# A first product of four batches in two levels: 49 quarter products for 56 in a graph network kernel

## The chip, the cores and the metric

The kernel runs on one core of a Trainium2 chip. The metric is the device time of one execution in microseconds; the median of three runs before the change is 1519.04 us.

## The reference

The input is x of shape (32, 512, 128): 32 batches, 512 nodes, 128 channels, all f32. Two layers follow each other.

```
# layer 0: both adjacency arguments are adj, so the K=7 taps fold to 4
x = layernorm(x + sum_k (adj^k x) W_k)          # k = 0..3
# layer 1: five steps of a gated unit over the graph
h = x
for 5 steps:
    m = adj @ h ; av = [m, m]
    u3 = h @ u3_w.T + u3_b
    z = sigmoid(av @ w3_w.T + w3_b + u3)
    r = sigmoid(av @ w4_w.T + w4_b + u3)
    hv = tanh(av @ w5_w.T + w5_b + (r*h) @ u5_w.T + u5_b)
    h = (1 - z)*h + z*hv
x = layernorm(x + h)
```

## The kernel before, in words

**Work and its order.** The batches are handled in 16 pairs. `pair(q, key0)` records all operations of pair q as `Op`s: the engine, a planned duration, what it comes after, which buffers it takes and gives back, and a key. `Plan.run` then plays these durations through once, while the program is built, and emits on each engine the ready operation with the smallest key that can take its buffers. The result is a fixed order for every engine; on the chip the engines run that order and wait on semaphores. Buffers come from the `slots` table (lines 153 to 172), so their counts shape the order as well. `KEYS` (line 24) holds the starting key of each pair, `LONG` (line 25) the step of the key from one of the five steps to the next, `inside` the number of pairs that may be under way.

**Products by seven.** A product of a 2x2 block matrix needs eight block products; the Winograd form needs seven and some sums. `seven` (line 358) issues the seven as PE groups into three PSUM banks. Banks `a` and `c` keep accumulating: after a group, its bank's sum is copied out (ACT) or added to something (DVE) before the next group may add to the same bank. `into` (line 344) says where the four output blocks go. The sums of the operands on the data side are made by POOL (`add`, line 475); those of the constant side (`T` for adj, `wt` for the weights, `at2S` for adj squared) are made once at the start.

**Layer 0** (`layer0`, line 530) of a pair has three such products. The first, through `pair_product` (line 479), is adj times x of the two batches: here the 2x2 blocks are the two batches against the two halves of the nodes. Each of the seven groups is two matmuls with a 128x128 stationary block and 256 moving columns (line 489), so 14 matmuls a pair. Its result goes to the tiles `tT`; x turned to channels goes to `xT`. The second product (line 567) takes `xT` and `tT` with the weights and writes `U` and `Y`. The third (line 626) applies adj squared to `U`, adds `Y`, and `norm` makes `h0`. From pair `FIRST` = 2 on, x and h0 are turned by `turn_nodes`, through DRAM; in pairs 0 and 1 by PE transposes (line 268).

**The five steps** (from line 778). Each step has u3 (line 785), the product with adj by `pair_product`, and the gates (lines 703 to 741). The new h is turned back for the next product by `turn` (line 310): a block transpose on DVE (line 325), four DMA pieces to DRAM (line 317) and one DMA back into `X` (line 323). `ON_PE` (line 23) names pairs whose last steps are turned by PE instead. All DMAs are issued by SP, in the planned order. After the last step POOL adds h to h0 (line 834), `norm` follows, and the result is stored (line 841). `h0` of a pair is thus held in SBUF through all five steps, for this residual. In a pair listed in `ON_PE` the last step is `finish` (line 743) instead, where PE does the sum.

Of the kernel before, what the change touches and what calls it, by code (L numbers as in the profile page):

```python
# [14 lines left out]
P = 128  # L15
# [7 lines left out]
ON_PE = {14: 1, 15: 3}  # L23
KEYS = [20.0, 58.0, 80.0, 110.0, 158.0, 194.0, 216.0, 246.0, 282.0, 312.0, 338.0, 366.0, 396.0, 432.0, 468.0, 480.0]
LONG = 20.0
FIRST = 2
EPS = 1e-5
# [95 lines left out]
def gnn_resnorm_kernel(  # L123
# [26 lines left out]
    def tiles(tag, n, shape=(P, N), pool=work):  # L150
# [4 lines left out]
        d=tiles("d", 6, (NR, R, NR, P), dram),  # L155
        xg=tiles("xg", 2, (P, 2, NK, P)),
        xT=tiles("xT", 4),
        tT=tiles("tT", 4),
        U=tiles("U", 3, (P, NK, 2, P)),
        Y=tiles("Y", 2, (P, 2, NK, P)),  # L160
        h0=tiles("h0", 5, (P, 2, NK, P)),
        hT=tiles("hT", 9),
        X=tiles("X", 5),
        uT=tiles("uT", 5),
        rh=tiles("rh", 4),
        z=tiles("z", 3),
        m=tiles("m", 7),
        S=tiles("S", 3, (P, 7, H, P)),
        v=tiles("v", 5),
        two=[None] * 3,  # L170
        inside=[None] * 10,
# [14 lines left out]
    T = const.tile([P, 4, H, HN], F32, tag="T", name="T")  # L186
    make_identity(nc, ident)
# [35 lines left out]


    w_of = lambda: plan["w0"].rearrange("p k b f -> p (k b f)")[:, : 7 * P]
    w0_in = plan("SP", 0.45, lambda: nc.sync.dma_start(w_of(), w0), take=[("U", "w0")], key=-70.0, late=6.5)

# [9 lines left out]

    w0_ready = plan("DVE", 2.3, layer0_weights, after=[w0_in], give=[("U", "w0")], key=-40.0)

# [289 lines left out]

    def layer0(q, key, entered):  # L530
# [3 lines left out]
        slots = [("S", f"Sx{q}")] + [("tT", f"tT{q}_{b}") for b in range(2)]  # L534
        dst = lambda i, j: plan[f"tT{q}_{i}"][:, j * HN : (j + 1) * HN]
        S_of = lambda i: plan[f"Sx{q}"][:, i]
        got, read = pair_product(lambda b: plan[xg][:, b], False, f"x{q}", dst, S_of, slots, ([xin[0]], [xin[1]]), key)
        read = read[0]
# [17 lines left out]

        U_done, reads, own = [], [], None
        for g in range(2):
            name = f"w{q}_{g}"
            block = lambda i, j, g=g: lambda: plan[f"{('xT', 'tT')[j]}{q}_{i}"][:, g * HN : (g + 1) * HN]  # L560
# [15 lines left out]
            t_in = [got[0][g], got[1][g]]  # L576
# [16 lines left out]
            def dst(i, j, g=g):  # L593
                if j == 0:
                    return plan[f"U{q}"][:, g * H : (g + 1) * H, i, :]
                return plan[f"Y{q}"][:, i, g * H : (g + 1) * H, :]
# [309 lines left out]
```

## Time and profile before

| what | value |
|---|---|
| median of 3 runs | 1519.04 us (1515.84 to 1519.85) |
| profiled execution | 1518.7 us |
| its span | 1516.9 us |
| PE busy | 1502.4 us (99%) |
| DVE busy | 968.9 us (64%) |
| POOL busy | 767.1 us (51%) |
| ACT busy | 750.4 us (49%) |
| hardware DMA queue | 127.93 MB, 31.7% of 16 engines |

The span is the time from the first to the last instruction in the trace of one execution. Busy time of an engine is the time in which at least one of its instructions runs. An f32 matmul leaves two records. The records of matmuls overlap, since they are pipelined, so what one costs is the distance from one start to the next. A group's mean duration says how long a single record lasts. In a line of the timeline the columns are start, duration, engine, line of the kernel, operation, output and input tiles, shapes, count; in square brackets stands how long the engine had been idle and what released it.

### The profile page before, as it was taken

How to read it: one execution, taken by the hardware profiler on the slowest of the kernel's cores; microseconds unless marked ns; L12 is line 12 of the kernel's file. 1: busy time of each engine (PE TensorE's matmuls, PEld its weight loads, DVE VectorE, ACT ScalarE, POOL GpSimd, SP SyncE). 2: the span in 40 equal slices, each digit the busy share in tenths (PEclk: the TensorE clock that was granted, in tenths of full speed). 3: DMA queues.
4: the chain of work that ended last, by engine and by line, in shares of the span. 5: the costliest groups of instructions: out<-in, count | busy, mean ns of one | idle time of the engine just before them, and what ended most of it. 6: DMA issues, size and time to landing. Idle time of an engine off the chain costs nothing.

```text
span 1516.9 us, 20326 instructions
## 1 busy us (share of the span) xinstructions
PE 1502.4 (99%) x6296; PEld 1044.2 (69%) x6296; DVE 968.9 (64%) x2048; ACT 750.4 (49%) x1610; POOL 767.1 (51%) x1082
## 2 busy tenths in 40 slices
PE   8999999999999999999999999999999999999997
PEld 7877666585678666677676767766666686756655
DVE  4455576757674766665776666577476657576665
ACT  3445444536554645445545445455455545555454
POOL 3654354446564645545555554555355564544351
PEclk9999999999999999999999999999999999999999
DMA  3133242334242424234333333334243222423310
GB/s 116 36 98 84 59 109 61 85 77 126 77 107 82 139 62 102 74 87 108 82 86 97 98 84 97 98 79 111 63 108 93 77 57 69 111 65 89 83 42 28
DMA packets 162140, 129.23 MB, mean 85 GB/s; under 512 B 18544, under 2 KB 127088, under 8 KB 162032
## 3 DMA queue, kind: packets, MB, share of 16 engines
q1 hardware_dynamic: 162032, 127.93, 31.7%
q8 instruction: 50, 0.82, 0.3%
q14 instruction: 58, 0.48, 0.1%
HBM read 64.95 MB, written 62.91 MB: 84 GB/s over the span
## 4 chain that ended last, share of the span: by engine, by line
PE 97%; DMA 1%; DVE 1%; POOL 1%; SPq 0%; issue 0%; ACT 0%; ACTq 0%; POOLq 0%; DVEq 0%
PE bank L489 38%; PE bank L703 36%; PE bank L785 9%; PE bank L567 6%; PE bank L626 6%; PE bank L425 1%; PE bank L751 1%; PE bank L268 1%; SPq L317 0%; DMA xg<-in_x 0%; DMA d<-v 0%; DMA v<-d 0%; DVE v L325 0%; POOL rstd L286 0%; DMA X<-d 0%
## 5 line engine op out<-in xcount | busy, mean ns | idle before, releaser
L489 PE MATMUL bank<-T,S 128*128 128x256 f32 x1400 | 346.8, 379 | 0.5 <-ACT tT L350 0.5
L740 POOL TENSOR_TENSOR hT<-z,hT 128x512 f32<-128x512 f32 x156 | 197.6, 1272 | 279.6 <-DVE z L738 277.7
L489 PEld LDWEIGHTS bank<-T,S 128*128 128x128 f32 x1400 | 262.7, 190 | 93.7 <-ACT m L350 35.9
L350 ACT COPY m<-bank 128x256 f32<-128x256 f32 x320 | 119.1, 372 | 266.3 <-PE bank L489 264.6
L489 PE MATMUL bank<-at,S 128*128 128x256 f32 x880 | 224.8, 379 | 1.1 <-ACT S L469 1.1
L354 DVE TENSOR_TENSOR m<-bank,m 128x256 f32<-128x256 f32 x240 | 100.4, 419 | 175.8 <-PE bank L489 116.8
L489 PEld LDWEIGHTS bank<-at,S 128*128 128x128 f32 x880 | 164.7, 190 | 63.0 <-issue 35.6
L736 DVE TENSOR_TENSOR bank<-bank,hT 128x512 f32<-128x512 f32 x156 | 107.5, 694 | 104.2 <-ACT bank L724 103.9
L703 PE MATMUL bank<-m,w4s 128*128 128x512 f32 x320 | 160.5, 592 | 0.0
L703 PE MATMUL bank<-m,w3s 128*128 128x512 f32 x320 | 159.4, 592 | 0.0
L724 ACT ACTIVATE bank<-bank,hv_b 128x512 f32<-128x512 f32 x160 | 105.6, 661 | 108.6 <-PE bank L703 107.5
L785 PE MATMUL bank<-hT,u3s 128*128 128x512 f32 x320 | 159.1, 592 | 0.0
L703 PE MATMUL bank<-m,w5s 128*128 128x512 f32 x320 | 156.9, 592 | 0.0
L703 PE MATMUL bank<-rh,u5s 128*128 128x512 f32 x320 | 156.9, 592 | 0.0
L708 DVE SCALAR_TENSOR_TENSOR bank<-bank,b4s,uT 128x512 f32<-128x512 f32 x160 | 119.9, 752 | 44.2 <-PE bank L703 37.2
L790 ACT ACTIVATE uT<-bank,ub3s 128x512 f32<-128x512 f32 x160 | 109.2, 686 | 64.3 <-PE bank L785 62.3
L710 ACT ACTIVATE bank<-bank 128x512 f32<-128x512 f32 x160 | 93.2, 583 | 92.4 <-DVE bank L708 92.3
L715 DVE SCALAR_TENSOR_TENSOR bank<-bank,b3s,uT 128x512 f32<-128x512 f32 x160 | 119.7, 753 | 27.2 <-PE bank L703 25.6
L717 ACT ACTIVATE z<-bank 128x512 f32<-128x512 f32 x160 | 95.0, 597 | 55.7 <-DVE bank L715 52.1
L325 DVE STREAM_TRANSPOSE v<-hT 128x512 f32<-128x512 f32 x152 | 105.7, 701 | 20.7 <-POOL hT L740 18.3
L711 DVE TENSOR_TENSOR rh<-bank,hT 128x512 f32<-128x512 f32 x160 | 108.0, 679 | 11.4 <-ACT bank L710 10.8
L738 DVE TENSOR_TENSOR z<-bank,z 128x512 f32<-128x512 f32 x156 | 104.9, 681 | 1.8
(129 smaller groups left out, 2190.8 us busy)
## 6 DMA issues: line engine op xcount, KB each, us to landing
d<-v SPq DMA_DIRECT2D x832, 64.0 KB, 1.8
X<-d SPq DMA_DIRECT2D x152, 256.0 KB, 2.8
v<-d SPq DMA_DIRECT2D x56, 256.0 KB, 2.8
xg<-in_x SPq DMA_DIRECT2D x32, 256.0 KB, 3.0
out<-h SPq DMA_DIRECT2D x32, 256.0 KB, 2.1
at<-in_adjT SPq DMA_DIRECT2D x4, 256.0 KB, 4.7
U<-in_w SPq DMA_DIRECT2D x1, 448.0 KB, 6.1
z<-in_w SPq DMA_DIRECT2D x3, 128.0 KB, 5.9
```

Source lines behind the costliest of these rows:

```text
L325: blocks = lambda: nc.vector.transpose(plan[f"v{name}"], src_of())
L350: return "ACT", COPY[cols], lambda src: nc.scalar.copy(dst(i, j), src)
L489: nc.tensor.matmul(dst, lhsT=left[:, k, :], rhs=right[:, k, :], start=(first and k == 0), stop=(last and k == H - 1), skip_group_check=True,)
L703: mm = lambda dst, w, src, first, last: nc.tensor.matmul(plan[dst], lhsT=w, rhs=plan[src], start=first, stop=last)
L708: emit = lambda: nc.vector.scalar_tensor_tensor(plan[pr], plan[pr], b4s, plan[uT], ALU.add, ALU.add)
L711: emit = lambda: nc.vector.tensor_tensor(plan[rh], plan[pr], plan[h], ALU.mult)
L715: emit = lambda: nc.vector.scalar_tensor_tensor(plan[pz], plan[pz], b3s, plan[uT], ALU.add, ALU.add)
L724: emit = lambda: nc.scalar.activation(plan[ph], plan[ph], AF.Tanh, bias=hv_b)
L736: emit = lambda: nc.vector.tensor_tensor(plan[ph], plan[ph], plan[h], ALU.subtract)
L740: emit = lambda: nc.gpsimd.tensor_tensor(plan[h], plan[z], plan[h], ALU.add)
L785: emit = lambda bn=bn, hb=h[b]: nc.tensor.matmul(plan[bn], lhsT=u3s, rhs=plan[hb], start=True, stop=True)
L790: emit = lambda bn=bn, uT=uT: nc.scalar.activation(plan[uT], plan[bn], AF.Identity, bias=ub3s)
```

## The change

The first product of layer 0 is made for two pairs, that is four batches, at a time from pair `SINGLE` = 2 on. The blocks are split twice: the outer level has seven products, of which each is again made by the seven scheme with 128x128 quarters, so 7 x 7 = 49 matmuls of 128 columns stand where 2 x 14 matmuls of 256 columns stood. Four of the outer products run together as batch A (one PSUM bank holds their four quarters of 128 columns), three as batch B. The inner sums lie in the new tiles `SA` and `SB`, those of the constant side in `TT`, made once on DVE. The outer sums of the results go to `M` and to a tile of the new tag `UY`, which replaces `U` and `Y`. Pairs 0 and 1 keep the old product, with its output in `M` instead of `tT`.

`h0` of pairs 0 to 12 is written to DRAM after the first step's product (`hd`) and read back in the last step for the residual. Several buffer counts, `ON_PE`, `KEYS` and `LONG` are changed with it. The diff, cut to its core:

```diff
 STEPS = 5
-ON_PE = {14: 1, 15: 3}
-KEYS = [20.0, 58.0, 80.0, 110.0, 158.0, 194.0, 216.0, 246.0, 282.0, 312.0, 338.0, 366.0, 396.0, 432.0, 468.0, 480.0]
-LONG = 20.0
+ON_PE = {14: 2, 15: 2}
+KEYS = [8.0, 22.0, 60.0, 88.0, 108.0, 144.0, 174.0, 188.0, 210.0, 244.0, 274.0, 310.0, 338.0, 368.0, 384.0, 396.0]
+LONG = 19.0
+KEPT = 3
 FIRST = 2
...
         bank=tiles("bank", 8, pool=psum),
         d=tiles("d", 6, (NR, R, NR, P), dram),
+        hd=tiles("hd", 6, (P, 2, NK, P), dram),
         xg=tiles("xg", 2, (P, 2, NK, P)),
-        xT=tiles("xT", 4),
-        tT=tiles("tT", 4),
-        U=tiles("U", 3, (P, NK, 2, P)),
-        Y=tiles("Y", 2, (P, 2, NK, P)),
-        h0=tiles("h0", 5, (P, 2, NK, P)),
-        hT=tiles("hT", 9),
-        X=tiles("X", 5),
-        uT=tiles("uT", 5),
-        rh=tiles("rh", 4),
+        xT=tiles("xT", 3),
+        M=tiles("M", 1, (P, 4, N)),
+        SA=tiles("SA", 1, (P, 25, P)),
+        SB=tiles("SB", 1, (P, 15, P)),
+        UY=tiles("UY", 2, (P, 4, N)),
+        h0=tiles("h0", 4, (P, 2, NK, P)),
+        hT=tiles("hT", 8),
+        X=tiles("X", 3),
+        uT=tiles("uT", 6),
+        rh=tiles("rh", 2),
         z=tiles("z", 3),
-        m=tiles("m", 7),
-        S=tiles("S", 3, (P, 7, H, P)),
-        v=tiles("v", 5),
+        m=tiles("m", 5),
+        S=tiles("S", 2, (P, 7, H, P)),
+        v=tiles("v", 4),
         two=[None] * 3,
-        inside=[None] * 10,
+        inside=[None] * 14,
     )
     plan = Plan(slots)
...
-    w_of = lambda: plan["w0"].rearrange("p k b f -> p (k b f)")[:, : 7 * P]
-    w0_in = plan("SP", 0.45, lambda: nc.sync.dma_start(w_of(), w0), take=[("U", "w0")], key=-70.0, late=6.5)
+    TT_sums = []
+    for i, n, of in (
+        (0, 4, lambda k, c: T[:, :, k, c]),
+        (4, 2, lambda k, c: at.rearrange("p (o k) c -> p o k c", o=2)[:, :, k, c]),
+        (6, 1, lambda k, c: at[:, H + k : H + k + 1, HN + c.start : HN + c.stop]),
+    ):
+        lo, hi = slice(0, P), slice(P, HN)
+        b11, b12, b21, b22 = of(0, lo), of(0, hi), of(1, lo), of(1, hi)
+        t = lambda j, i=i, n=n: TT[:, i : i + n, j, :]
+        def emit(b11=b11, b12=b12, b21=b21, b22=b22, t=t):
+            for j, (a, b) in enumerate(((b12, b11), (b22, t(0)), (b22, b12), (b21, t(1)))):
+                nc.vector.tensor_tensor(t(j), a, b, ALU.subtract)
...
+    def quad_product(X_of, name, after, key):
+        SA, SB, PA, M = (f"{t}{name}" for t in ("SA", "SB", "PA", "M"))
+        X = lambda i, j, b: lambda: X_of(2 * i + b)[:, j * H : (j + 1) * H]
+        LOW, HIGH = slice(3, 5), slice(5, 7)
+        part = lambda S, at, w: lambda: plan[S][:, at + w.start : at + w.stop]
+        def inner(S, at, a, after):
+            out = lambda i: lambda: plan[S][:, at + i]
+            s2 = add(0.45, out(1), a(0, 0), a(1, 0), ALU.subtract, after, key)
+            s0 = add(0.45, out(3), a(1, 0), a(1, 1), ALU.add, after, key)
+            s1 = add(0.45, out(0), out(3), a(0, 0), ALU.subtract, [s0], key)
+            s3 = add(0.45, out(2), a(0, 1), out(0), ALU.subtract, [s1], key)
+            return s1, s2, s3, s0
+        quarter = lambda i, j: lambda b, k: lambda: X_of(2 * i + b)[:, j * H + k]
+        at_of = {0: 4, 1: 11, 2: 18}
+        own = plan("-", 0.0, lambda: None, after=[o for a in after for o in a], take=[("SA", SA), ("UY", PA)], key=key)
+        s0, s2, s1 = [], [], []
+        for b, w in ((0, HIGH), (1, LOW)):
+            s0.append(add(0.73, part(SA, 11, w), X(1, 0, b), X(1, 1, b), ALU.add, [own], key))
+            s2.append(add(0.73, part(SA, 4, w), X(0, 0, b), X(1, 0, b), ALU.subtract, [own], key))
+            s1.append(add(0.73, part(SA, 18, w), part(SA, 11, w), X(0, 0, b), ALU.subtract, s0[-1:], key))
+        x11 = inner(SA, 0, quarter(0, 0), [own])
+        q = lambda i: lambda: plan[SA][:, 4:].rearrange("p (o b) c -> p o b c", o=3)[:, :, i]
+        ready = s0 + s1 + s2
+        i2 = add(0.98, q(1), q(5), q(3), ALU.subtract, ready, key)
+        i0 = add(0.98, q(3), q(3), q(4), ALU.add, [i2], key)
+        i1 = add(0.98, q(0), q(3), q(5), ALU.subtract, [i0], key)
+        i3 = add(0.98, q(2), q(6), q(0), ALU.subtract, [i1], key)
+        def lefts(S, at, direct):
+            sums = {2: 0, 4: 1, 6: 2, 3: 3}
+            if direct is None:
+                sums = {**sums, 5: 4, 0: 5, 1: 6}
+            return [
+                (lambda i=i: plan[S][:, at + sums[i]])
+                if i in sums
+                else direct(*{0: (0, 0), 1: (0, 1), 5: (1, 1)}[i])
+                for i in range(7)
+            ]
+        def right(block, sums):
+            quarters = {0: (0, 0), 1: (1, 0), 6: (1, 1)}
+            def R_of(i):
+                if i in quarters:
+                    k, c = quarters[i]
+                    return block[:, k, c * P : (c + 1) * P]
+                return TT[:, sums, {2: 1, 3: 0, 4: 2, 5: 3}[i]]
+            return R_of
+        def product(dst, left, i, first, last):
+            for o, (L, R_of) in enumerate(left):
+                nc.tensor.matmul(
+                    dst[:, o],
+                    lhsT=L[i](),
+                    rhs=R_of(i),
+                    start=(first and o == 0),
+                    stop=last,
+                    skip_group_check=True,
+                )
+        def terms(factors, waits):
+            return [(lambda: factors, lambda i=i: i, list(waits.get(i, ()))) for i in range(7)]
+        block = lambda i, j: slice((2 * i + j) * P, (2 * i + j + 1) * P)
+        shape = lambda n: lambda bank: bank[:, : n * P].rearrange("p (o c) -> p o c", o=n)
+        factors = [
+            (lefts(SA, 0, quarter(0, 0)), right(B11, 4)),
+            (lefts(SA, 4, None), right(T[:, 2], 2)),
+            (lefts(SA, 11, None), right(T[:, 0], 0)),
+            (lefts(SA, 18, None), right(T[:, 1], 1)),
+        ]
+        waits = {2: [x11[0], i1], 3: [x11[3], i0], 4: [x11[1], i2], 6: [x11[2], i3]}
+        dst = lambda i, j: plan[PA][:, :, block(i, j)]
+        own = plan("-", 0.0, lambda: None, after=ready, take=[("SB", SB), ("M", M)], key=key)
+        p, ends = seven(
+            f"{name}A", ready + TT_sums, 0.88, terms(factors, waits), product, into(dst, N), key, shape(4)
+        )
+        pA = p
+        x12 = inner(SB, 0, quarter(0, 1), [own])
+        x22 = inner(SB, 4, quarter(1, 1), [own])
+        s3 = [add(0.73, part(SB, 8, HIGH), X(0, 1, 0), part(SA, 18, HIGH), ALU.subtract, [own, *s1], key)]
+        one = slice(4, 5)
+        last = lambda: X_of(1)[:, H + 1 : H + 2]
+        s3.append(add(0.45, part(SB, 8, one), last, part(SA, 18, one), ALU.subtract, [own, *s1], key))
+        four = slice(0, 4)
+        all4 = list(x12) + [i0, i1, i2, i3]
+        s3.append(add(1.27, part(SB, 8, four), part(SB, 0, four), part(SA, 18, four), ALU.subtract, all4, key))
+        plan("-", 0.0, lambda: None, after=pA + s3, give=[("SA", SA)], key=key)
+        factors = [
+            (lefts(SB, 0, quarter(0, 1)), right(B21, 5)),
+            (lefts(SB, 4, quarter(1, 1)), right(T[:, 3], 3)),
+            (lefts(SB, 8, None), right(B22, 6)),
+        ]
+        dstB = lambda i, j: plan[M][:, :3, block(i, j)]
+        plus = lambda i, j: plan[PA][:, :3, block(i, j)]
+        pB, endsB = seven(
+            f"{name}B",
+            s3 + list(x22) + ends,
+            0.66,
+            terms(factors, {}),
+            product,
+            into(dstB, 3 * P, plus),
+            key,
+            shape(3),
+            give=[("SB", SB)],
+        )
+        def dve(d, a, b, after):
+            emit = lambda: nc.vector.tensor_tensor(d(), a(), b(), ALU.add)
+            return plan("DVE", 0.69, emit, after=after, key=key)
+        PA_of = lambda o: lambda: plan[PA][:, o]
+        M_of = lambda o: lambda: plan[M][:, o]
+        u = dve(PA_of(3), PA_of(3), PA_of(0), ends)
+        v = dve(M_of(3), PA_of(1), PA_of(2), ends + [own])
+        e22 = dve(M_of(3), M_of(3), PA_of(3), [u, v])
+        e12 = dve(M_of(2), M_of(2), PA_of(3), [u] + endsB)
+        e21 = dve(M_of(1), M_of(1), PA_of(3), [u] + endsB)
+        plan("-", 0.0, lambda: None, after=endsB + [e12, e21, e22], give=[("UY", PA)], key=key)
+        read = pA + pB + s3 + list(x11 + x12 + x22) + s0 + s1 + s2
+        return [endsB + [e12], endsB + [e12], [e21, e22], [e21, e22]], [read] * 4
+    in_quad, t_reads = {}, {}
     def layer0(q, key, entered):
         xin = x_in.get(q) or loaded_x(q, (key, key))
         xg = f"xg{q}"
-        slots = [("S", f"Sx{q}")] + [("tT", f"tT{q}_{b}") for b in range(2)]
-        dst = lambda i, j: plan[f"tT{q}_{i}"][:, j * HN : (j + 1) * HN]
-        S_of = lambda i: plan[f"Sx{q}"][:, i]
-        got, read = pair_product(lambda b: plan[xg][:, b], False, f"x{q}", dst, S_of, slots, ([xin[0]], [xin[1]]), key)
-        read = read[0]
+        quad = q >= SINGLE
+        Mn = f"Mx{q - (q - SINGLE) % 2 if quad else q}"
+        if not quad:
+            dst = lambda i, j: plan[Mn][:, i, j * HN : (j + 1) * HN]
+            S_of = lambda i: plan[f"Sx{q}"][:, i]
+            slots = [("S", f"Sx{q}"), ("M", Mn)]
+            got, read = pair_product(
+                lambda b: plan[xg][:, b], False, f"x{q}", dst, S_of, slots, ([xin[0]], [xin[1]]), key
+            )
+            read = read[0]
+        else:
+            if Mn == f"Mx{q}":
+                other = x_in[q + 1] = loaded_x(q + 1, (key, key))
+                X_of = lambda b: plan[f"xg{q + b // 2}"][:, b % 2]
+                in_quad[q] = quad_product(X_of, f"x{q}", [[o] for o in xin + other], key)
+            i = 2 * ((q - SINGLE) % 2)
+            got, read = (o[i : i + 2] for o in in_quad[q - i // 2])
+            got, read = list(got), read[0] + read[1]
+        def t_block(b, g):
+            if not quad:
+                return plan[Mn][:, b, g * HN : (g + 1) * HN]
+            return plan[Mn][:, 2 * g + (q - SINGLE) % 2, b * HN : (b + 1) * HN]
         x_turned = []
         for b in range(2):
...
+        flat = lambda i: plan[f"UY{q}"][:, 2 * i : 2 * i + 2].rearrange("p k f -> p (k f)")
+        U_of = lambda: flat(0).rearrange("p (k b c) -> p k b c", k=NK, b=2)
+        Y_tile = lambda: flat(1).rearrange("p (b k c) -> p b k c", b=2, k=NK)
         U_done, reads, own = [], [], None
         for g in range(2):
             name = f"w{q}_{g}"
-            block = lambda i, j, g=g: lambda: plan[f"{('xT', 'tT')[j]}{q}_{i}"][:, g * HN : (g + 1) * HN]
+            block = lambda i, j, g=g: lambda: (
+                t_block(i, g) if j else plan[f"xT{q}_{i}"][:, g * HN : (g + 1) * HN]
+            )
             S = lambda i, name=name: lambda: plan[f"S{name}"][:, i].rearrange("p k c -> p (k c)")
             W = lambda i: lambda: wc[:, i, :]
             WT = lambda i: lambda: wt[:, i, :]
...
-            t_in = [got[0][g], got[1][g]]
-            take = [("S", f"S{name}")] + ([("U", f"U{q}"), ("Y", f"Y{q}")] if g == 0 else [])
+            t_in = list(got[0]) + list(got[1]) if quad else [got[0][g], got[1][g]]
+            take = [("S", f"S{name}")] + ([("UY", f"UY{q}")] if g == 0 else [])
             own = plan("-", 0.0, lambda: None, after=x_turned + t_in + [w0_ready, own], take=take, key=key + 8)
             s2 = add(0.73, S(2), block(0, 0), block(1, 0), ALU.subtract, [own], key + 8)
...
             reads += p + [s2, s3]
-        give = [(t, f"{t}{q}_{b}") for t in ("xT", "tT") for b in range(2)]
-        plan("-", 0.0, lambda: None, after=reads, give=give, key=key)
+        plan("-", 0.0, lambda: None, after=reads, give=[("xT", f"xT{q}_{b}") for b in range(2)], key=key)
+        if not quad or Mn != f"Mx{q}":
+            plan("-", 0.0, lambda: None, after=reads + t_reads.pop(Mn, []), give=[("M", Mn)], key=key)
+        else:
+            t_reads[Mn] = reads
         name = f"y{q}"
-        block = lambda i, j: lambda: plan[f"U{q}"][:, i * H : (i + 1) * H, j, :]
+        block = lambda i, j: lambda: U_of()[:, i * H : (i + 1) * H, j, :]
         S = lambda i: lambda: plan[f"Sy{q}"][:, i]
...
             got, read = pair_product(X_of, turned, name, dst, S_of, slots, after, key)
+            if s == 0 and q < NP - KEPT:
+                emit = lambda: nc.sync.dma_start(plan[f"hd{q}"], plan[f"h0{q}"])
+                done = read[0] + read[1] + h_done[0] + h_done[1]
+                t = plan("SP", 0.45, emit, after=done, take=[("hd", f"hd{q}")], key=key + 5, late=2.5)
+                spilt = plan("-", 0.0, lambda: None, after=[t], give=[("h0", f"h0{q}")], key=key)
+            if last and q < NP - KEPT:
+                emit = lambda: nc.sync.dma_start(plan[f"h0{q}"], plan[f"hd{q}"])
+                take, give = [("h0", f"h0{q}")], [("hd", f"hd{q}")]
+                fetched = plan("SP", 0.45, emit, after=[spilt] + got[0], take=take, give=give, key=key + 5, late=3.0)
             if s > 0:
                 for b in range(2):
...
                 )
-                t = plan("POOL", 1.27, emit, after=[t], give=[("X", Xb)], key=key + 17)
+                ready = [t, fetched] if q < NP - KEPT else [t]
+                t = plan("POOL", 1.27, emit, after=ready, give=[("X", Xb)], key=key + 17)
                 i = 2 * q + b
                 y_of = lambda k, y=y: y()[:, k, :]
                 over = norm(NK, f"1_{i}", y_of, y_of, [t], [], key + 17)
```

## The prediction

> **What bounds the kernel now.** I read the page's busy shares first, then the table by stage, then PE's waits, then stretches of PE's timeline for the price of each matmul shape.
>
> ```profile
> PE 1502.4 (99%) x6296; PEld 1044.2 (69%) x6296; DVE 968.9 (64%) x2048; ACT 750.4 (49%) x1610; POOL 767.1 (51%) x1082
> PE 97%; DMA 1%; DVE 1%; POOL 1%; SPq 0%; issue 0%; ACT 0%; ACTq 0%; POOLq 0%; DVEq 0%
> ```
>
> PE is busy 99% of the span and is 97% of the chain that ended last. Where PE is not busy shows in the stage table (window, PE busy and records, then the other engines):
>
> ```profile
> 0.00:12.00 12.00, 7.60 (x27) 6.26 (x28) 3.21 (x6) 3.65 (x6) 3.96 (x10) 1.00 0.68 213
> 50.00:100.00 50.00, 48.39 (x280) 39.47 (x279) 25.95 (x75) 23.94 (x54) 28.90 (x47) 1.00 0.22 59
> 100.00:1400.00 1300.00, 1300.00 (x5342) 893.51 (x5341) 849.54 (x1778) 654.50 (x1410) 673.80 (x944) 1.00 0.34 89
> 1500.00:1517.00 17.00, 8.80 (x51) 6.14 (x49) 9.54 (x29) 7.01 (x16) 2.92 (x6) 0.92 0.16 62
> ```
>
> From 100 to 1400 us PE never stops, at full clock. All idle time is 4.4 us while x arrives, 1.6 us between 50 and 100, 0.4 near 1430, and 8.2 us after the last matmul: 14.5 us. PE's waits agree:
>
> ```profile
> PE bank L268 <- DMA xg<-in_x: 4.4, 2, 3.8
> PE bank L489 <- ACT S L469: 1.1, 1, 1.1
> PE bank L489 <- ACT tT L350: 0.5, 1, 0.5
> PE bank L268 <- POOL hT L740: 0.4, 1, 0.4
> ```
>
> So PE's work in the middle is worth its full time, and other engines' work is worth nothing until it makes PE stop.
>
> The price of a matmul is its pitch, not its mean duration (379 ns and 275 ns overlap their neighbours). Each f32 matmul leaves two records, so x4 of 128x256 are two matmuls and x8 of 128x128 are four, both 512 columns:
>
> ```profile
> 420.03 1.03 PE L489 MATMUL bank<-at,S 128*128 128x256 f32 x4
> 420.90 1.05 PE L626 MATMUL bank<-U,at 128*128 128x128 f32 x8
> 421.79 1.03 PE L489 MATMUL bank<-at,S 128*128 128x256 f32 x4
> 422.65 1.05 PE L626 MATMUL bank<-U,at 128*128 128x128 f32 x8
> 423.54 1.95 PE L626 MATMUL bank<-S,at2S 128*128 128x128 f32 x16
> ```
>
> Start to start: 0.865 us for two 256-column matmuls (0.4325 each), 0.89 us for four of 128 (0.2225 each).
>
> **The change part by part.**
>
> *The matmuls.* Two pairs' first products are 2 x 14 = 28 matmuls of 256 columns: 28 x 0.4325 = 12.11 us. A group of four batches now issues 49 of 128 columns: 49 x 0.2225 = 10.90 us. That is 1.21 us less per group; pairs 2 to 15 make 7 groups: 8.5 us. Columns alone (one eighth fewer) would give 10.5 us; two microseconds go back because short matmuls have the worse pitch. The built program has 343 matmuls at the new line and 196 fewer at L489 (1344 to 1148), so it does what it says; every other kind is unchanged in number.
>
> Here a rule speaks against the change. The trace has 111 ns per 128-column record and 216 ns per 256-column record: halving costs 3%. The Trainium skill ("TensorE: Matmul & The Clock Gate", section "Back-to-back issue gap") gives a stream of weight load and matmul at N=128 about 81 ns each, where the isolated gap is 56 ns, so weight loads should cost 45% more. Estimated by that page, the 49 would cost 49 x 0.4325/2 x 1.45 = 15.4 us, and the change would lose 23 us in all. L626 loads a new 128x128 weight for each 128-column matmul, just as the new product does, and runs at 0.89 us for four. I take the row.
>
> *POOL.* Removed per group: 8 sums of 256 columns at 0.73 = 5.8 us. Added: 25 sums. The rows give 0.73 for 256 columns and 1.27 for 512; on that line 128 cost 0.46 and 384 cost 1.0 (estimates). 7 x 0.73 + 13 x 0.46 + 4 x 1.0 + 1.27 = 16.4 us. So 10.6 more, 74 us over 7 groups: POOL goes from 767 to about 841 us, 56% of the span.
>
> *DVE and ACT.* Removed per group: 6 DVE sums at 0.419 and 8 ACT copies at 0.372. Added: 3 sums of 512 columns out of PSUM (0.69), 7 of 384 (between the 0.42 and 0.69 rows: 0.555), 5 of 512 with both sources in SBUF, and 4 ACT copies at 0.586. The 5 have two prices. Alone such a sum takes 0.68; beside a POOL sum the trace shows
>
> ```profile
> 7.22 1.42 POOL L476 TENSOR_TENSOR S<-xg 128x256 f32<-128x256 f32 x2 [5.93 <-DMA xg<-in_x]
> 7.92 1.27 DVE L220 TENSOR_TENSOR T<-at 128x512 f32<-128x512 f32 x1 [7.06 <-DMA at<-in_adjT]
> 8.60 1.17 POOL L476 TENSOR_TENSOR S<-S,xg 128x256 f32<-128x256 f32 x1
> ```
>
> 1.27 and 1.17 where 0.68 and 0.73 are usual. The Trainium skill ("GPSIMD Engine Reference", section "1. Specifications") says that GpSimd shares its SBUF interfaces with VectorE and meets contention when a DVE instruction has two SBUF inputs; the rows agree. So the 5 cost 3.4 to 6.4 us per group and hold POOL about as much. DVE rises by 48 to 69 us, plus 12 sums for the constant TT once (6 to 8 us, in the first 40 us): about 1030 of 1510 us, 68%. ACT falls by 4. No engine nears PE; I cost all this at nothing between 100 and 1400, because there PE has other pairs' products and gates to issue. What is late if that cover fails is a bank of the long product: its accumulation waits for a 512-column copy (0.59) where it waited for 0.37.
>
> *DRAM for h0.* 13 writes and 13 reads of 512 KB, 13.6 MB on 128; DMA share from 32% to about 35%. No row has this size in the steady state: 256 KB lands in 2.1 to 3.0 us, 448 KB in 6.1 in the crowded start. I take 4, as the two 256 KB rows with their fixed part shared, and keep 2.1 and 6.1. SP issues 26 more at about 0.45: 12 us on a queue that mostly waits (562 us for L325 alone). The read is issued after the last step's first output block and used by the residual sum after gates and turn. The turn alone is 0.70 + 1.76 + 1.8 + 0.35 + 2.8 = 7.4 us, with some 9 us of gates before it, so 4 or 6 us hide. The residual sum on POOL (L834) now waits for this read too; behind it in POOL's order stand other pairs' sums for their next products. Queued behind a late write or read on SP are the turns (L317, L323) of other pairs, for which the next product's copies and sums wait.
>
> *A longer wait.* The second product of either pair (L567) now waits for batches A and B of four batches and the outer sums, not for one pair's seven groups; `SA`, `SB` and `M` exist once, so the next group waits for both pairs' second products. Who waits for that is layer 0 of four batches, while the steps of earlier pairs fill PE; nothing, as long as the keys keep it ahead.
>
> *Fewer buffers, moved starts.* X 5 to 3, rh 4 to 2, m 7 to 5, S 3 to 2, h0 5 to 4. Fewer buffers (all counts in the diff) tie PE's order to later releases. In the new order I followed each release to the PE work that stands before its user at the prices above: away from the ends the shortest distances are the same as before (a copy of 0.37 behind one matmul group), and those gave no wait in the trace. Nothing, then, up to 3 us.
>
> *The start.* Here I charge something. Pairs 0 and 1 now start 14 us apart (before 38), and the first group at key 60. After the last matmul of pair 0's third product only 20 matmuls of 128 columns stand before the transposes of its normalised h0: 4.45 us. In the profile that way took from 52.4 us (the product's end) to 59.6 (the sixth L296): 7.2 us. So 2.7 us of PE idle; before, PE idled 1.6 in that region, and part of it may not return. +1 to +2.7; I take +1.5. TT and the weights are ready before their first users.
>
> *The tail.* ON_PE keeps four steps with PE transposes in all, so PE's count is the same. Pair 15 turns one step more by DMA (7.4 us against about 1.5); pair 14's products and gates, interleaved with it in the new order, stand over that. After the last u5 product five groups of four 128-column matmuls (5 x 0.89) follow in both versions. The two batches' final sums now end back to back instead of 1.8 us apart, so the first statistics start 0.9 later and the last end 0.9 later (8 x 0.4 us on DVE, to 1510.55 before). The batch that ends last is now the one scaled on DVE (1.4 on POOL, 1.33 on DVE) and no longer the one on POOL and ACT (1.8 and 1.5 after the statistics). 0, plus or minus 1.
>
> **Sum.** -8.5 + 1.5 + 0.5 (stray waits) = -6.5. The profiled execution took 1518.7 us (span 1516.9 and 1.8 around it) and is 0.3 below the median, 1519.04. Forecast 1518.7 - 6.5 + 0.3 = 1512.5.
>
> **The rivals.**
>
> *The start costs nothing* (0.15): the first pairs idle as little as before or less, and the saving is whole: 8.5 to 10, so 1509 to 1510.5. For: the start had 1.6 us idle to win. Against: the 20 matmuls above.
>
> *Stray waits eat it* (0.17): fewer buffers, and 512-column copies between accumulations of one bank, give short stops. At 0.3 to 0.9 us per group of four (7 groups), 2 to 6.5 us go and a gain of 0 to 4.5 is left: 1514.5 to 1519. For: POOL and DVE each gain 5% load, and POOL already waits on transfers. Against: 0.00 idle from 100 to 1400 under the same kind of tight places.
>
> *SP's queue becomes the limit* (0.06), slower: a 512 KB write waits on SP for the release of h0's readers, or a read for a free h0 of 4, and the turns of other pairs queue behind. Each of 26 issues would have to stop PE by more than (8.5 - 1.5 + 4.6)/26 = 0.45 us to pass the bound of slower. At 6.1 us landing and 0.8 us of PE each, 21 us lost less 7 won: 1533. Against: SP waits for its producers most of the time, and most turns have over 10 us of PE work between landing and user.
>
> **How the numbers follow.** The likeliest case (0.62) is 1510.5 to 1514.5. 0.3% (4.6 us, about what a measurement of this kernel can tell from no change) puts faster below 1514.5: 0.62 + 0.15 = 0.77; same 0.17; slower 0.06. The range 1508 to 1518 takes in the whole saving with a better start and most of the stray waits.
>
> **What would show it.** PE busy near 1494; four new matmuls at 0.89 us; PE 0.0 idle from 100 to 1400; 3 us idle between 40 and 80; POOL near 840. It is wrong if the four take over 0.95, if PE waits for X, m or SA in the middle, or if PE waits follow the 512 KB transfers.

## Result and the profile after

The changed kernel takes 1511.33 us (median of 5 runs, 1510.59 to 1512.27) where the kernel before takes 1519.04 (5 runs beside it): ratio 0.9955, 95% interval 0.9941 to 0.997. It is 7.7 us faster; the forecast was 6.5. The profiled execution after took 1511.12 us with a span of 1509.3.

The page's busy shares and its chain of what ended last:

```profile
PE 1493.1 (99%) x6590; PEld 1044.1 (69%) x6590; DVE 1021.8 (68%) x2123; ACT 749.1 (50%) x1582; POOL 844.3 (56%) x1201
PE 97%; DMA 1%; DVE 1%; SPq 0%; POOL 0%; ACT 0%; issue 0%; POOLq 0%; DVEq 0%
```

PE is still the bound. It has 294 records more and 9.3 us of busy time less. POOL (predicted 841) and DVE (about 1030) took up the sums. The stage table (window, PE busy and records, PEld, DVE, ACT, POOL, clock, DMA share, GB/s):

```profile
0.00:12.00 12.00, 8.28 (x41) 6.45 (x42) 4.19 (x7) 4.69 (x8) 5.44 (x11) 1.00 0.69 213
12.00:50.00 38.00, 35.68 (x228) 32.62 (x228) 26.01 (x60) 10.08 (x24) 18.49 (x21) 1.00 0.19 56
50.00:100.00 50.00, 48.57 (x279) 38.41 (x277) 26.63 (x68) 26.75 (x57) 37.40 (x62) 1.00 0.23 64
100.00:1400.00 1300.00, 1299.93 (x5657) 901.33 (x5656) 897.62 (x1850) 655.05 (x1386) 742.43 (x1052) 1.00 0.37 99
1500.00:1510.00 10.00, 0.68 (x7) 0.49 (x5) 4.23 (x20) 1.51 (x4) 2.94 (x6) 0.77 0.16 62
```

The middle stays full: 0.07 us idle in 1300. What is new is 2.3 us of idle time between 12 and 50, where the kernel before had 0.02:

```profile
12.00:50.00 38.00, 37.98 (x237) 34.98 (x236) 19.49 (x43) 11.73 (x28) 17.62 (x24) 1.00 0.24 70
```

PE's waits after the change name it (total us, times, longest):

```profile
PE bank L290 <- DMA xg<-in_x: 4.5, 2, 3.6
PE bank L749 <- DVE UY L376: 1.3, 1, 1.3
PE bank L749 <- ACT UY L372: 0.9, 2, 0.5
PE bank L290 <- ACT h L318: 0.4, 1, 0.4
```

The second wait for x (1.0 us at 14) is pair 1's, whose start moved forward. The second product's wait of 1.3 at 27 us is for an add on DVE, which stands in DVE's queue behind four sums for `TT`; the last of them, the add, and PE's matmul:

```profile
25.82 0.94 DVE L241 TENSOR_TENSOR TT<-at,TT 128x256 f32<-128x256 f32 x1
26.68 0.41 DVE L376 TENSOR_TENSOR UY<-bank,UY 128x256 f32<-128x256 f32 x1
27.24 0.68 PE L749 MATMUL bank<-wc,S 128*128 128x128 f32 x4 [1.34 <-DVE UY L376]
```

The two ACT waits are one bank's copies between groups of pair 1's second product, issued back to back. The transposes of h0 wait 0.4.

The new product on PE's timeline, eight records (four matmuls) of 128 columns, and what follows:

```profile
78.58 1.05 PE L615 MATMUL bank<-TT,SA 128*128 128x128 f32 x8
79.47 1.02 PE L888 MATMUL bank<-rh,u5s 128*128 128x512 f32 x2
```

79.47 - 78.58 = 0.89 us, as L626 in the kernel before. The unseen costs, from the groups by shape (busy, mean ns) and the DMA issues (count, size, median us to landing):

```profile
L498 POOL TENSOR_TENSOR SA<-SA 128x384 f32<-128x384 f32 x28 | 28.1, 1003 | 0.7
L672 DVE TENSOR_TENSOR M<-M,UY 128x512 f32<-128x512 f32 x21 | 17.4, 856 | 0.2
hd<-h SPq DMA_DIRECT2D x13, 512.0 KB, 3.9
h<-hd SPq DMA_DIRECT2D x13, 512.0 KB, 3.9
```

### The profile page after: what moved, and what is told of

Same layout as the page of the kernel before. It is cut to its first block, busy times and chain, and to the rows that moved or that the text cites. A ratio compares the mean times of both kernels' runs of the same rounds, so it can differ in the third digit from the quotient of the medians.

```text
span 1509.3 us, 21208 instructions
## 1 busy us (share of the span) xinstructions
PE 1493.1 (99%) x6590; PEld 1044.1 (69%) x6590; DVE 1021.8 (68%) x2123; ACT 749.1 (50%) x1582; POOL 844.3 (56%) x1201
## 4 chain that ended last, share of the span: by engine, by line
PE 97%; DMA 1%; DVE 1%; SPq 0%; POOL 0%; ACT 0%; issue 0%; POOLq 0%; DVEq 0%
PE bank L888 36%; PE bank L511 32%; PE bank L970 9%; PE bank L811 7%; PE bank L749 6%; PE bank L615 5%; PE bank L936 1%; PE bank L447 1%; DMA z<-in_w 0%; PE bank L290 0%; DMA X<-d 0%; DVE TT L241 0%; DMA xg<-in_x 0%; POOL S L498 0%; ACT h L318 0%
## 5 line engine op out<-in xcount | busy, mean ns | idle before, releaser
L511 PE MATMUL bank<-T,S 128*128 128x256 f32 x1232 | 307.1, 379 | 0.2
L511 PEld LDWEIGHTS bank<-T,S 128*128 128x128 f32 x1232 | 228.4, 190 | 75.3 <-ACT m L372 32.0
L511 PE MATMUL bank<-at,S 128*128 128x256 f32 x824 | 211.3, 379 | 0.0
L511 PEld LDWEIGHTS bank<-at,S 128*128 128x128 f32 x824 | 153.4, 190 | 57.4 <-issue 36.7
L376 DVE TENSOR_TENSOR UY<-bank,UY 128x256 f32<-128x256 f32 (+1 forms) x117 | 54.4, 467 | 82.0 <-PE bank L749 36.2
```

The source lines that it names most:

```text
L376: return "DVE", ADD[cols], lambda src: nc.vector.tensor_tensor(dst(i, j), src, dst(i, j), ALU.add)
L511: nc.tensor.matmul(dst, lhsT=left[:, k, :], rhs=right[:, k, :], start=(first and k == 0), stop=(last and k == H - 1), skip_group_check=True,)
```

## Experiments

Twelve kernels ran in three sets. Each has its ratio to the kernel before measured beside it, whose median was 1519.28, 1519.64 and 1519.19 in the three; the last column is the median less 1511.59, the changed kernel's own in the first set.

| kernel | set | median us | ratio to before, 95% | to the changed kernel |
|---|---|---|---|---|
| before_again | 1 | 1519.26 | 1.0002 (0.9993 to 1.001) | +7.7 |
| after_again | 1 | 1511.59 | 0.9946 (0.9934 to 0.9959) | 0 |
| split | 1 | 1530.45 | 1.007 (1.0057 to 1.0084) | +18.9 |
| single | 1 | 1530.15 | 1.0067 (1.0053 to 1.0081) | +18.6 |
| single_oldkeys | 2 | 1535.77 | 1.0108 (1.0093 to 1.0123) | +24.2 |
| keep | 2 | 1532.70 | 1.0093 (1.0079 to 1.0107) | +21.1 |
| spblock | 2 | 1517.93 | 0.9989 (0.9981 to 0.9998) | +6.3 |
| cover | 2 | 1575.68 | 1.0374 (1.0359 to 1.0388) | +64.1 |
| cover_pool | 3 | 1553.51 | 1.0225 (1.0211 to 1.0239) | +41.9 |
| cover_planned | 3 | 1528.22 | 1.0054 (1.0042 to 1.0067) | +16.6 |
| tt_late | 3 | 1519.05 | 0.9999 (0.9991 to 1.0007) | +7.5 |
| start | 3 | 1517.38 | 0.9992 (0.9984 to 1.0001) | +5.8 |

One number besides the views is used below, the *excess*: over all neighbouring matmul records, the time from start to start beyond the median of that line and shape, where it is more than 5 ns. It counts stops, a slow start and broken pace alike. It is 8.1 us before, 8.2 in before_again, 8.2 after and 8.8 in after_again.

**Both kernels again.** before_again and after_again are the two files unchanged.

> The kernel before, once more, for a second trace of its start. Theory (the start differs from run to run): its matmuls in the first 12 us ran at half pace until about 11 us in the first trace and until 6.7 in the trace of after; that is a matter of when the clock rises and not of the kernel, so this trace may show either, and the time goes with it by 1 to 3 us (1516 or 1519). Rival (the order of the start sets it): the second trace shows the half pace until 11 us again.

> The changed kernel, once more. Theory: PE busy 1493 to 1496 by how long the start runs at half pace, the idle of about 7.5 us before 100 us again with the same two stops (near 14 and 27 us), 1511 plus or minus 1.5. Rival (those stops are chance): idle before 100 us falls to the 6.0 of before.

The gain returns (7.7 us between medians). before_again ran at half pace only until 8.7 us where before did until 12.3 (the expectation had read 11), so this differs from run to run. The spans of the two are equal, 1516.9, but by two differences that cancel: before_again loses 2.0 us less in the first 12 us and 1.8 more between 100 and 1400.

In after_again PE stops for the same second product on DVE's `UY` (1.2), the same two ACT copies (0.9) and `h` (0.4); the stop for pair 1's x does not return, and PE's idle time in the first 100 us is 6.6 us, between the 7.5 expected and the rival's 6.0. The stops that return belong to the order, the x stop to the run.

**split: what a shorter matmul costs.** Each of the 1148 matmuls of 256 columns at L511 is issued as two of 128, same columns, one weight load more each.

```
 for k in range(H):
-    nc.tensor.matmul(dst, lhsT=left[:, k, :], rhs=right[:, k, :], ...)
+    for c in range(H):
+        nc.tensor.matmul(dst[:, chunk(c)], lhsT=left[:, k, :], rhs=right[:, k, chunk(c)], ...)
```

> Prices the shape by itself: every matmul of 256 columns in the steps' products and in pairs 0 and 1 becomes two of 128 with the same weights loaded twice; columns and results are the same. 1148 matmuls become 2296. Theory (a 128-column matmul has a pitch of 0.2232 and a 256-column one of 0.4322): 1148 x 0.0142 = 16.3 us more, 1527 to 1529. Rival (a weight load for each 128 columns costs 45%): over 1148 x 0.19 = 220 us more, 1730.

It is 18.9 us slower, 1.5 us above the range of the theory, and 17.7 by the spans of the profiled executions: 15.4 to 16.5 ns for each split, about 4% of a 256-column matmul. The page:

```profile
PE 1511.2 (99%) x8886; PEld 1123.2 (74%) x8886; DVE 1020.6 (67%) x2123; ACT 749.2 (49%) x1582; POOL 842.3 (55%) x1201
```

The weight loads rise only to 74% busy and stay hidden. By the stream of the Trainium skill ("TensorE: Matmul & The Clock Gate", section "Back-to-back issue gap"), 81 ns at 128 columns where the isolated gap is 56, 45% more, an estimate for this run is some 220 us; here the measurement decides, as the row did in the forecast.

**single: the old product inside the new kernel.** `SINGLE` = 16 sends every pair through `pair_product`; the tiles `SA` and `SB` go, `M` gets a second buffer, all else (keys, buffers, h0 in DRAM) stays.

> Undoes the products alone: every pair makes its first product by the old 14 matmuls of 256 columns; the keys, ON_PE, h0 in DRAM and the smaller buffers stay as in after (M twice, since a pair needs its own). Theory (the gain is PE's columns at their pitch): PE busy 8.2 more than after, time 1519 to 1521. Rival (the new order and buffers give part of the gain): clearly under 1517. Second rival (the old product fits these keys badly): idle between 100 and 1400, over 1524.

The second rival came true: 18.6 us slower. The excess is 19.3 where after_again has 8.8, so 10.5 us are stops and broken pace, and 8.2 of the 18.7 between the spans are left for the columns, the product's own difference. What is left is by the meaning of the excess no more than the counts times the usual distances, so it is no second proof of the forecast's 8.5; the distances themselves are what split tests. But the old product in these surroundings is 11 us slower than in the kernel before.

**single_oldkeys: single with the old schedule.** Also takes the start keys, `LONG`, `ON_PE` and the limit of pairs inside from the kernel before.

> The old first product everywhere, with the old keys, LONG, ON_PE and the limit of 10 pairs, but with the smaller buffers and with h0 in DRAM as in after. The run single lost 11 us to stops of PE that after doesn't have. Theory (those stops come from keys that were chosen for groups of four; buffers and DRAM cost nothing): 1518 to 1521, and PE's stops between 100 and 1400 under 2 us. Rival (fewer buffers stop PE when the short products don't relieve it): over 1524, with waits for m, S or X in the middle.

1535.8, slower still by 5.6. My theory that the keys alone made single slow fell. The rival's time came (over 1524), not its place: of an excess of 26.3, 12.2 us lie between 50 and 100 us. The old keys were chosen for the old buffers; with the new, fewer ones and the trip to DRAM they stop PE more. Which of these does it was not separated.

**keep: h0 not sent to DRAM.** `KEPT` = 16, with the same 4 buffers of h0, no tile `hd`.

> h0 stays in SBUF for all pairs (no write to DRAM, no read back) with the four h0 buffers of after. What DRAM is for: with h0 kept, at most four pairs are between layer 0's end and their store. Theory (the transfers cost nothing and buy buffers): slower than after, since a pair of the next group must wait with its third product until an older pair has stored: 3 to 20 us. Rival (the transfers cost time, or the fifth buffer isn't needed): equal or faster, 1508 to 1512.

21 us slower, just beyond the theory's 3 to 20. PE is idle 4.2 us between 100 and 400 and 2.8 between 1450 and 1500, and its waits are many small ones:

```profile
PE bank L510 <- ACT m L371: 3.7, 8, 0.5
PE bank L289 <- POOL hT L924: 3.5, 2, 1.9
PE bank L748 <- ACT UY L371: 2.8, 6, 0.5
```

As I read them: a pair that waits for an h0 buffer starts late, fewer pairs are on the way, and PE runs one pair's groups back to back, where each waits for the copy before it; that chain was not traced. With these keys and four buffers of h0, the changed kernel without the trip to DRAM is slower than the kernel before.

**spblock: SP held up.** Each of the 13 reads of h0 is issued twice, so SP waits for the first to land before the second.

```
+nc.sync.dma_start(plan[f"h0{q}"], plan[f"hd{q}"])
 nc.sync.dma_start(plan[f"h0{q}"], plan[f"hd{q}"])
```

> The rival of the SP queue: each of the 13 reads of h0 is issued twice in a row into the same buffer, so the second waits on SP for the first to land (about 4 us), with all other transfers behind it. PE's order is unchanged. Theory (the turns behind it have mostly over 10 us until their users): under 2 us slower than after, 1511 to 1513.5. Rival (SP's queue is near its limit): 13 x 4 us x some part reaches PE, 10 us or more slower, over 1521.

6.3 us slower, between the two. SP's own waits show the block, 46.2 us in 13 times, 3.6 on average:

```profile
SPq L990 <- DMA h<-hd: 46.2, 13, 5.1
```

PE then waits in two places more, L511 on `m` (2.4) and on `S` (2.0), where the changed kernel has none. By which of the queued transfers each came late was not traced, and the doubled reads also move 6.8 MB more, which was not separated from the block. 6.3 / 13 = 0.5 us for each read: of 46 us of block most is absorbed, not all.

**cover: do the sums have room?** In the outer step of each group, `s0` and `s2` are computed three times over on POOL and `v` five times on DVE. PE's order is the same, and the planner is not told.

```
-s0.append(add(0.73, part(SA, 11, w), X(1, 0, b), X(1, 1, b), ALU.add, [own], key))
+s0.append(add(0.73, part(SA, 11, w), X(1, 0, b), X(1, 1, b), ALU.add, [own], key, 3))
 ...                                  # s2 likewise, v five times
```

> Takes away cover: in each group of four the four outer sums s0 and s2 run three times on POOL (8 more of 256 columns, 5.8 us per group) and one outer result sum runs five times on DVE (4 more of 512 columns, 2.7 to 5 us per group), with the same results and the same order on all engines. POOL about +41 us, DVE about +20 to 35. Theory (only PE's columns count; the sums have room): time within 1.5 us of after, 1511 to 1513. Rival (the sums' load is near what stops PE): 3 to 8 us slower than after.

64 us slower, though POOL has only 43 us more work and DVE 24, and POOL stays at 56%:

```profile
PE 1515.7 (96%) x6590; PEld 1054.9 (67%) x6590; DVE 1045.3 (66%) x2151; ACT 748.5 (48%) x1582; POOL 887.6 (56%) x1257
```

The theory fell, and so did the rival's 3 to 8 us. PE's waits:

```profile
PE bank L514 <- DVE m L376: 9.4, 3, 4.8
PE bank L976 <- POOL hT L931: 7.6, 2, 4.0
PE bank L514 <- POOL S L500: 6.4, 3, 5.3
PE bank L618 <- DVE M L373: 6.2, 3, 2.3
```

Only the fourth is the new product. The others are older steps of other pairs, on engines that now run late. Why there is no room shows when one group's stretch is cut out of the stage table, first in the changed kernel, then in cover:

```profile
505.00:532.00 27.00, 27.00 (x142) 20.97 (x141) 12.86 (x26) 14.96 (x34) 26.56 (x44) 1.00 0.51 135
532.00:570.00 38.00, 38.00 (x165) 25.96 (x165) 28.18 (x59) 19.73 (x40) 17.30 (x24) 1.00 0.32 85
```

```profile
539.00:564.00 25.00, 22.47 (x127) 17.86 (x126) 10.36 (x22) 9.29 (x21) 24.77 (x41) 1.00 0.40 115
```

While the four batches' sums run, POOL is full: 26.56 of 27 us, the group's 25 sums laced with those of other pairs; afterwards it is at 46%. PE stays full in the changed kernel, since the order has each sum done when its user comes. In cover POOL works 41 us without a break of 0.4 us (523 to 564) where it was 35 (497 to 532), and PE loses 2.5 us in the part that is shown.

**cover_pool and cover_planned: load, or the plan's ignorance?** The first keeps only POOL's repeats. The second has all of cover's repeats, and tells the planner their length (`us * times` on POOL, `0.69 * times` on DVE), so that it writes another order.

> Only POOL's part of cover, not planned for: s0 and s2 three times each, 56 sums of 256 columns more, some 43 us over the run; DVE as in the changed kernel. If it is POOL's queue, in which work of other stages stands behind the bursts of sums, that made cover slow, then 1550 to 1576 us, most of cover's 64 us over the changed kernel. If it was DVE's burst of five sums (3.4 us more before the next copy out of PSUM), 1512 to 1525 us.

> The same extra sums as in cover (the outer sums s0 and s2 three times each on POOL, the outer result sum v five times on DVE), about 43 us more on POOL and 24 us more on DVE over the run, but their full length is told to the planner, which writes another order. Theory, the order that the planner wrote is what hides the sums: with the load known it finds an order that hides it, 1512 to 1520 us, and the stops of PE between 100 and 1400 us add up to less than 8 us. Rival, the load itself is too much, because POOL's sums come in chains that PE's first products wait for: within 15 us of cover's 1576 us. In between, 1520 to 1560, both have a part.

POOL alone costs 41.9 us, two thirds of cover's loss. Told of all of it, the planner gives back 47.5 of 64.1 us; 16.6 stay. PE's stops between 100 and 1400 are then 9.2 us, against the 8 that I had allowed and 37.6 in cover. So both have a part: most of the cover is the order, and the rest is load that no order found here hides. The pages, and the stretch from 50 to 100 us (here PE busy, clock, DMA share, GB/s), of cover_pool and then of cover_planned:

```profile
PE 1512.0 (97%) x6590; PEld 1054.2 (68%) x6590; DVE 1021.6 (66%) x2123; ACT 747.5 (48%) x1582; POOL 882.5 (57%) x1257
50.00:100.00 50.00, 43.24 (x236) 0.93 0.12 35
```

```profile
PE 1500.6 (98%) x6590; PEld 1047.1 (69%) x6590; DVE 1037.9 (68%) x2151; ACT 748.0 (49%) x1582; POOL 881.8 (58%) x1257
50.00:100.00 50.00, 47.45 (x274) 1.00 0.21 64
```

POOL's busy time in cover_pool is 38 us more than in the changed kernel (882.5 for 844.3), but the loss is not that time passed on one for one. In the profiled execution, whose span is 45.7 us longer, PE's idle time, the span less its busy time, rises by 26.8 us (43.0 for 16.2), and its busy time by 18.9 (1512.0 for 1493.1) with the same 6590 records. Part of the 18.9 is the clock. It stands at 0.93 in the row where the changed kernel has 1.00: in the trace it is at half speed at six places, for 3.4 or 6.8 us each, beside stops of PE of 1.5 to 5.3 us, and the matmuls there lose about 14 us. cover has eight such places, 15 us; the changed kernel and cover_planned have none after the start. A long stop of PE thus cost more here than its own length.

**tt_late and start: the new stops at the start.** In tt_late the sums that fill `TT` move behind `at2S`'s on DVE; in start pair 1's x is also asked for right after pair 0's.

```
-TT_sums.append(plan("DVE", ..., emit, after=T_sums, key=22.0))
+TT_sums.append(plan("DVE", ..., emit, after=T_sums + A2_sums, key=45.0))
...                                   # and in start:
-x_in = {0: first_x()}
+x_in = {0: first_x(), 1: loaded_x(1, (-58.0, -58.0))}
```

> The sums of parts of T and at that fill TT, 5.7 us of DVE, move behind DVE's earlier setup sums (those that feed PE's first matmuls), and the planner writes a new order for the first 140 of PE's groups. Theory, they stood in DVE's queue ahead of the adds out of PSUM that PE waits for: the stop of 1.2 to 1.3 us at 27 us (the second product waiting for DVE's UY) goes, 1510.3 us, 1.0 to 1.3 us below the changed kernel. Rival, the start is bound by DVE's whole work and the stop moves to another place: within 0.5 us of the changed kernel's 1511.5 us.

> As tt_late, and x of pair 1 is asked for right behind x of pair 0. Theory: besides the stop at 27 us the one of about 1.0 us at 14 us (transposes of pair 1 waiting for xg) goes too, 1509.5 us, about 2 us below the changed kernel, and the fastest of all. Rival, x of pair 1 takes the DMA engines from x of pair 0 and from the weights, and PE's first transposes start later: the gain of tt_late is lost, 1511 us or above, with a longer first wait of PE for xg.

Both theories fell: 7.5 and 5.8 us are lost. The rivals do not fit either: tt_late is far outside 0.5 us, and in start the first wait for x is no longer than before (3.5 us for 3.6). The stop on `UY` shrinks from 1.3 to 0.7, and larger ones come. The first `TT` sums on DVE's timeline begin, in the changed kernel and then in tt_late, with

```profile
15.73 0.68 DVE L241 TENSOR_TENSOR TT<-T 128x512 f32<-128x512 f32 x1
16.45 0.69 DVE L241 TENSOR_TENSOR TT<-T,TT 128x512 f32<-128x512 f32 x1
```

```profile
38.73 1.21 DVE L480 TENSOR_TENSOR TT<-T 128x512 f32<-128x512 f32 x1
39.98 1.10 DVE L480 TENSOR_TENSOR TT<-T,TT 128x512 f32<-128x512 f32 x1
43.27 0.41 DVE L355 TENSOR_TENSOR v<-bank,UY 128x256 f32<-128x256 f32 x1
```

Early, POOL is mostly idle and those of 512 columns take 0.68; late, they run beside POOL's sums at 1.1 to 1.2. (Those of 256 columns have it the other way round, 0.9 early and 0.42 late; all twelve take about 7.6 us in both.) Late, they stand ahead of an add of pair 0's third product, and PE waits 0.6 us for that. The largest stop has another cause. The end of pair 0's third product and the first transpose of its h0 on PE's timeline, in the changed kernel and then in tt_late:

```profile
47.90 1.06 PE L811 MATMUL bank<-UY,at2S 128*128 128x128 f32 x8
55.10 0.33 PE L290 MATMUL bank<-ident,h 128*128 128x128 f32 x1
```

```profile
49.17 1.06 PE L809 MATMUL bank<-UY,at2S 128*128 128x128 f32 x8
52.68 0.61 PE L747 MATMUL bank<-wt,S 128*128 128x128 f32 x4
56.63 0.33 PE L272 MATMUL bank<-ident,h 128*128 128x128 f32 x1 [3.34 <-ACT h L300]
```

From the one to the other it is 7.2 us in the changed kernel and 7.5 in tt_late, so the way to h0 is hardly longer. But the order that the planner wrote leaves PE only until 53.3 us with other work, where the changed kernel's has work up to 55.1; hence 3.34 us of stop for 0.4. The same stop of 3.34 us stands in start. Beside it the clock falls, for 3.4 us in tt_late and for 6.8 in start, which costs about 1.6 and 3.0 us of matmul time. The stretch from 50 to 100 us of the two:

```profile
50.00:100.00 50.00, 45.93 (x264) 0.97 0.20 57
50.00:100.00 50.00, 46.27 (x261) 0.93 0.20 59
```

start is 1.7 us faster than tt_late, and PE's wait for x is 4.1 us for 5.2; since that wait was 4.5 and 3.5 in two runs of the changed kernel, these traces do not show that the earlier request did it. With `TT` left in its place it might gain something; it wasn't tried. No kernel tried beats the changed one.

## Why the prediction was right, and where not

**The matmuls: right, 8.2 for 8.5.** The mean from start to start, without the distances that hold a stop or the half pace of the start, is 216.1 ns at 256 columns, before and after, and 111.6 ns at 128. 392 records fewer of the one and 686 more of the other give 84.7 - 76.6 = 8.15 us. The 8.5 came from distances rounded to 10 ns. That the weight loads of short matmuls cost 3 to 4% and not 45% is shown by split.

**The start: right size in the table, wrong places.** Idle time in the first 100 us rises from 6.03 to 7.47 us: +1.4 for the 1.5 forecast. That they are so close is luck: after_again has 6.63. The way to pair 0's h0 is as forecast: 7.1 us from its third product's end (48.8) to the second transpose (55.87), with 20 matmuls in between, and PE loses about 2.5 us there, in two bank copies (0.9, and slow restarts after them) and 0.4 at the transposes. But the kernel before lost as much in that region, so it adds next to nothing (idle 50 to 100 us: 1.61 before, 1.43 after), and the sign "3 us idle between 40 and 80" did not come (1.4). The added cost lies where the forecast put nothing. The failed step is "TT and the weights are ready before their first users": `TT` is ready, but its sums, and the others of the setup, stand in DVE's queue before an add that PE needs (1.3). The x of pair 1 (1.0, in one of two runs) is the rest. The half pace of the first matmuls moves the sum as well: it ended at 12.3 us in before and at 6.8 in after. So the excess of the first 100 us went only from 7.4 to 7.9 us, and to 8.6 in after_again, whose half pace lasted until 11.6; from 12 us on it rose by 2.8 and 1.2 us.

**Stray waits and the tail.** Stray waits: 0.07 us between 100 and 1400 for 0.5. The tail after the last matmul is 8.6 us for 8.1: +0.5, within 0 plus or minus 1.

**The sum.** -8.2 by pitch, +0.1 (after) or +0.6 (after_again) of excess, +0.5 of tail: -7.6 or -7.1. The spans fell by 7.6 and 7.1. So the gain lies in the counts alone: with the new order, buffers and trip to DRAM PE loses as much to stops as before, or up to 0.6 more. The forecast's -6.5 is a microsecond short: the start, the stray waits and the tail together cost 0.6 (after) or 1.1 (after_again) where 2.0 was charged, and the matmuls gave 0.3 less.

**The unseen prices.** 384-column sums: 1.00 on POOL (1.0 taken), 0.55 out of PSUM (0.555). Sums of 512 columns with both sources in SBUF: 0.86 to 0.99, between the bounds 0.68 and 1.27. 512 KB: 3.9 us to land (4 taken).

**"No engine nears PE": right outcome, wrong reason.** POOL's 74 us more were costed at nothing because 56% looked like room, with other pairs' PE work as cover. cover and cover_pool refute that as a reason: 38 us on the same engine, at the same share, cost 42. The share is a mean over stretches as unlike as the two shown, 98% and 46%. The sums are free because each stands in the order where its user comes late enough; cover_planned, where knowing the load gave back 47.5 of 64.1 us, supports this, and shows that such an order hides most, and not all, of more.

**Buffers and SP.** "Nothing, up to 3 us" for fewer buffers held for the kernel as it is, with its own keys. It is no property of the buffers: the same buffers with the old product lose 11 us against the kernel before, with the old keys 16, and without the DRAM trip the changed kernel loses 21. The slower rival, SP as the limit, set 0.45 us of PE stop for each issue as its turning point. spblock comes to 0.5 for each of 13 reads, 0.24 over the 26 issues, so a held-up SP does reach PE, but with 3.6 us of block for each read it comes to half of what the rival needed. In the changed kernel the new transfers land in 3.9 us, and PE is idle 0.07 us between 100 and 1400.

## What to carry to other kernels

A matmul saving is best priced by start-to-start distance for each shape; here, with PE full, it arrived whole. An engine's share over the whole run says nothing on whether work added to it is free: cut out the stretch in which it is added, and ask whether the order was written with that work in it. A stop of the full engine can cost more than its length, so compare its busy time for the same work too. Keys, buffer counts and a trip to DRAM can be one design, of which no part can be judged by undoing it alone.

## What was not expected of the hardware

- TensorE began at half pace, by a time that differs from run to run: 128-column records about 0.21 us apart until 12.3 us into the span (before), 8.7 (before_again), 6.8 (after) and 11.6 (after_again). The clock column shows 1.00 for these stretches, but the trace's record of the clock begins only where the pace doubles, so that 1.00 is no measurement. The Trainium skill ("TensorE: Matmul & The Clock Gate", Part 1 on the clock gate) has about 3.4 us of this, and a count that varies by run; here it is 3.3 to 8.5 us from the first matmul.
- The clock fell to half again beside stops of 1.5 to 5.3 us (keep, spblock, tt_late, start, cover, cover_pool), for 3.4 or 6.8 us each time, which cost 1.2 to 3.2 us of matmul time. In single it fell beside four stops of 0.45 us within 4 us. The changed kernel's stops of up to 1.3 us had no such effect in two traces.
- Repeated sums on POOL, 38 us more of its busy time at a mean share of 57%, cost the kernel 42 us. In the profiled execution it was 46, of which PE stood idle for 27 and ran at a slower pace for the rest.
